# Splitting matmuls into 32-column tiles in a masked graph-attention layer

## The chip, the core and the metric

The kernel runs on one NeuronCore of a Trainium2 chip. The core has a matrix engine (TensorE, "PE" in the profile, whose weight loads stand apart as "PEld"), a vector engine (VectorE, "DVE"), an activation engine (ScalarE, "ACT"), a general engine (GpSimd, "POOL") and a sequencing engine that issues DMAs here (SyncE, "SP"). The metric is the device time of one execution in microseconds (us). The kernel before takes 3434.6 us (median of 5 runs, 3427.57 to 3441.34).

## The reference

The input x has 8 graphs of 2048 nodes and 256 channels in fp32; adj is a 2048 x 2048 integer matrix. One attention layer with 8 heads of 32 channels is followed by a feed-forward step, with three layer norms:

```python
qkv = einsum('fnc,ck->fnk', x, w_qkv); q, k, v = split(qkv, 3)
scores = einsum('fnhd,fmhd->fhnm', q, k) / sqrt(32)
scores = where(adj > 0, scores, -1e9)
attn = softmax(scores)
t = einsum('fhnm,fmhd->fnhd', attn, v)
y = layernorm(x + t) * g1 + be1
h = relu(y @ w1 + b1)
z = layernorm(y + h @ w2 + b2) * g2 + be2
out = layernorm(x + z)
```

All matrices of the layer are fp32 in the kernel as well, and all of its large products are fp32 matmuls.

## The kernel before, in words

**Items.** The attention is cut into 1024 items: 8 graphs (f), 4 chunks of 512 queries (qc), 2 groups of 4 heads (g) and 16 blocks of 128 keys (mb). All engines have their orders written out in one Python loop; no scheduler moves anything afterwards. In step t of the loop the kernel issues, in this order: one piece of other work (`advance`), the exponentials of item t + 1, the scores of item t + 2 (`LEAD = 2`), the values of item t, and the sums of its denominators (`add_up`).

**Scores** (L204 to L222). K and Q are held with channels on partitions, 32 channels to a head. For each of the four heads one product takes 32 rows of K (one head) by 128 keys as weights and streams the 512 queries: the result has 128 keys on partitions and 512 queries in a bank of PSUM. Two heads share a pair of banks. There are three pairs, used in turn, and an item takes two; so the scores of the next item can start when VectorE has read the first pair of the item before. VectorE adds the mask (L220, two instructions of 128 x 1024 an item) and writes the result to a buffer p in SBUF.

**Exponentials** (L224): one ScalarE instruction of 128 x 2048 an item, in place.

**Values** (L236): four products an item, one a head. The weights are 128 keys by 32 channels, and the result of head h goes to partitions 32h to 32h + 31 of one bank, which gathers over the 16 key blocks. The bank is one of two x banks, which change sides with every (f, qc, g).

**Denominators.** GpSimd (L258) and accumulating DMAs that GpSimd issues (L255) add up the exponentials of 16 items into four tiles; four products with a matrix of ones then sum over keys (L294, 128 rows by 32 columns each).

**Other work.** Generators hold the rest: transposes of x (`turn_rows`, L151), projections to Q and K (`channels`, L174) and V (`project`, L199), denominators (L294, L301), the division (L330), and a tail with layer norms, transposes (L396) and the feed-forward products (L409, L421). `advance` gives one piece of it to each step, between the values of one item and the scores of the next; a piece takes the free x bank. `MORE` marks a place where a piece may be cut in two. In the order of TensorE's work an item is therefore: scores, values, at most one such piece.

**Shapes on TensorE.** The scores use 32 rows by 128 columns of the array, the values and the ones 128 rows by 32 columns; projections, feed-forward products and transposes the whole 128 x 128.

The products in question, with the lines of the profile, and what calls them:

Of the kernel before, what the change touches and what calls it, by code (L numbers as in the profile page):

```python
# [19 lines left out]
P = 128  # L20
H = 8
D = 32
# [17 lines left out]
def stats(nc, small, t, mhalf):  # L40
    st = small.tile([P, nc.vector.BN_STATS_DIM], F32, name="st")
    nc.vector.bn_stats(st, t)
    mv = small.tile([P, nc.vector.BN_AGGR_DIM], F32, name="mv")
    nc.vector.bn_aggr(mv, st)
    rs = small.tile([P, 1], F32, name="rs")
    nc.gpsimd.tensor_scalar(rs, mv[:, 1:2], EPS, 1.0, op0=ALU.add, op1=ALU.mult)
    nc.gpsimd.tensor_tensor(rs, rs, mhalf, ALU.pow)
    return mv, rs


def normalize(nc, dst, t, mv, rs):
# [4 lines left out]
def fast_path(ctx, tc, cst, x, adj, out, RS):  # L56
    nc = tc.nc
    F, N, C = x.shape
    NCK, TPC, MB = N // CH, CH // P, N // P
# [19 lines left out]
    ident, identb, wqkv, w1s, w2s = cst["ident"], cst["identb"], cst["wqkv"], cst["w1s"], cst["w2s"]  # L79
    state = {"pair": 0, "side": None, "turn": 0, "turned": False, "holder": None, "tails": 0}  # L80

    def score_pair():
        i = state["pair"]
        state["pair"] = (i + 1) % 3
        return ps_s[i].tile([P, 2, CH], F32, name=f"s{i}")

    def bank(dt=F32):
        shape = [P, CH] if dt == F32 else [P, 2, CH]
        if state["side"] is not None:
            i = 1 - state["side"]  # L90
            return ps_x[i].tile(shape, dt, name=f"x{i}")
        i = state["turn"]
        state["turn"] = (i + 1) % 5
        pool = ps_s[i] if i < 3 else ps_x[i - 3]
        return pool.tile(shape, dt, name=f"s{i}" if i < 3 else f"x{i - 3}")
# [9 lines left out]
    def give(t):  # L105
        live[:] = [None if u is t else u for u in live]
# [32 lines left out]
    QT, KT, V, XT = {}, {}, {}, {}  # L139
    XD = [dp.tile([NCK, P, 2, CH], F32, name=f"xd{f}") for f in range(F)]  # L140

    def queries(f, c, xT):
        for g in range(2):
            yield from channels(QT, qp, "qT", (f, c, g), xT, g * P)
# [23 lines left out]
    def channels(store, pool, name, key, xT, k0):  # L168
        yield BANK
        ps = bank()  # L170
        for a in range(2):
            if a:
                yield MORE
            nc.tensor.matmul(ps, wqkv[:, a, k0:k0 + P], xT[:, a, :], start=(a == 0), stop=(a == 1))  # L174
        store[key] = pool.tile([P, CH], F32, name=name)
        nc.scalar.copy(store[key], ps)  # L176

    def reload(f, c):
        while (f, c) not in XT:
            yield 1  # L180
        yield INPUTS - 1
        xT = take([P, 2, CH], F32)
        nc.sync.dma_start(xT, XD[f][c])
        yield 3
        return xT

    def project(f, c, g, xT=None):
        if xT is None:
            xT = yield from reload(f, c)
            while len(KT) < (2 * f + g) * NCK + c:  # L190
                yield 1
        yield from channels(KT, kp, "kT", (f, c, g), xT, C + g * P)
        yield BANK
        ps = bank()
        for j in range(TPC):
            if j == TPC // 2:
                yield MORE
            for a in range(2):
                nc.tensor.matmul(ps[:, j * P:(j + 1) * P], xT[:, a, j * P:(j + 1) * P],  # L199
                                 wqkv[:, a, 2 * C + g * P:2 * C + (g + 1) * P], start=(a == 0), stop=(a == 1))  # L200
        v = vp.tile([P, TPC, P], F32, name="v")
        nc.scalar.copy(v, ps.rearrange("p (j c) -> p j c", c=P))
        V[f, c, g] = v
        give(xT)  # L204
# [4 lines left out]
    def scores(item):  # L209
        f, qc, g, mb = item  # L210
        pt = PT[item] = pp.tile([P, 4, CH], F32, name="p")
        ps2 = [score_pair() for _ in range(2)]

        for half in (1, 0):
            for j in range(2):
                r = D * (2 * half + j)
                nc.tensor.matmul(ps2[half][:, j, :], KT[f, mb // TPC, g][r:r + D, (mb % TPC) * P:(mb % TPC + 1) * P],  # L217
                                 QT[f, qc, g][r:r + D, :], start=True, stop=True)
        for half, ps in enumerate(ps2):
            nc.vector.tensor_tensor(pt[:, 2 * half:2 * half + 2, :], ps,  # L220
                                    MK[f, qc, mb // 2][:, mb % 2, None, :].to_broadcast([P, 2, CH]), ALU.add)
# [57 lines left out]
    def rows(v):  # L279
        return v[:, None, :].to_broadcast([P, TPC, C])  # L280
# [54 lines left out]
    def tail(f, qc, y, xin):  # L335
        yield from norm(y)
        yield from feed_forward(y)
        yield 1
        z = y
        yield from norm(z)  # L340
        nc.gpsimd.tensor_tensor(z, z, rows(cst["g2r"]), ALU.mult)  # L341
        yield 1
        nc.gpsimd.tensor_tensor(z, z, rows(cst["be2r"]), ALU.add)  # L343
        yield 1
        nc.gpsimd.dma_start(z, xin, accum_op=ALU.add)
        yield 7
        yield from norm(z)
        nc.sync.dma_start(out[f, qc * CH:(qc + 1) * CH, :].rearrange("(p j) c -> p j c", p=P), z)
        state["tails"] -= 1
# [20 lines left out]
    def finish(f, qc):  # L370
        y = yp.tile([P, TPC, C], F32, name="y")
        xr, xb = state["rows"], take([P, TPC, C], F32)
        yield from divide(f, qc, y)
        nc.vector.tensor_tensor(y, y, xr, ALU.add)
        norm_halves(y)
        nc.vector.tensor_tensor(xb, xr, rows(cst["be2r"]), ALU.add)
        yield from feed_forward(y)
        z = y
        norm_halves(z)
        for h in range(0, TPC, 2):  # L380
            nc.vector.tensor_tensor(z[:, h:h + 2], z[:, h:h + 2], rows(cst["g2r"])[:, h:h + 2], ALU.mult)
            nc.vector.tensor_tensor(z[:, h:h + 2], z[:, h:h + 2], xb[:, h:h + 2], ALU.add)
        norm_halves(z)
        dst = out[f, qc * CH:(qc + 1) * CH, :].rearrange("(p j) c -> p j c", p=P)
        for h in range(0, TPC, 2):
            nc.sync.dma_start(dst[:, h:h + 2], z[:, h:h + 2])

    def feed_forward(y):
        yield TURNED
        state["turned"] = True  # L390
        yT = work.tile([P, 2, CH], F32, name="turned")
        for a in range(2):
            yield BANK
            ps = bank()
            for j in range(TPC):
                nc.tensor.transpose(ps[:, j * P:(j + 1) * P], y[:, j, a * P:(a + 1) * P], ident)  # L396
            nc.scalar.activation(yT[:, a, :], ps, AF.Identity, bias=cst["be1c"][:, a:a + 1], scale=cst["g1c"][:, a:a + 1])
        yield 1
        nc.gpsimd.tensor_tensor(y, y, rows(cst["g1r"]), ALU.mult)
        yield 1  # L400
        nc.gpsimd.tensor_tensor(y, y, rows(cst["be1b2r"]), ALU.add)
        hT = work.tile([P, 2, CH], F32, name="hT")
        for d in range(2):
            yield BANK
            ps = bank()
            for a in range(2):
                if a:
                    yield MORE
                nc.tensor.matmul(ps, w1s[:, a, d * P:(d + 1) * P], yT[:, a, :], start=(a == 0), stop=(a == 1))  # L409
            nc.scalar.activation(hT[:, d, :], ps, AF.Relu, bias=cst["b1s"][:, d:d + 1], scale=1.0)  # L410
        state["turned"] = False
        yield 1
        z = y
        for jj in range(0, TPC, 2):
            yield BANK
            ps = bank()
            for j in range(jj, jj + 2):
                if j > jj:
                    yield MORE
                for d in range(2):  # L420
                    nc.tensor.matmul(ps[:, (j - jj) * C:(j - jj + 1) * C], hT[:, d, j * P:(j + 1) * P], w2s[:, d, :],  # L421
                                     start=(d == 0), stop=(d == 1))
            nc.vector.tensor_tensor(z[:, jj:jj + 2, :], ps.rearrange("p (b c) -> p b c", c=C), z[:, jj:jj + 2, :], ALU.add)


# [18 lines left out]
    def advance(t, free=True, finish=False):  # L444
# [18 lines left out]
        while state["holder"] and (finish or late and state["holder"][2] == MORE):  # L463
# [4 lines left out]


    NEXT = {(1, 1): [(turn, 0)], (3, 1): [(turn, 1)], (3, 10): [(project, 0, 0)], (5, 1): [(turn, 2)],  # L470
            (5, 8): [(project, 1, 0)], (6, 0): [(turn, 3)], (6, 4): [(project, 2, 0)], (6, 8): [(project, 3, 0)],
            (6, 12): [(project, 0, 1)], (7, 0): [(project, 1, 1)], (7, 4): [(project, 2, 1)], (7, 8): [(project, 3, 1)]}

    def begin():
# [324 lines left out]
```

## Time and profile before

| what | value |
|---|---|
| median of 5 runs | 3434.6 us |
| the profiled execution | 3435.5 us |
| its span, from the first to the last instruction | 3433.7 us |
| TensorE, share of the span | 93% |
| VectorE | 80% |
| GpSimd | 75% |
| ScalarE | 71% |
| granted clock of TensorE, share of full speed | 0.986 |
| DMA engines, 100 to 3380 us | 76% busy |

A group of the profile is written as line, engine, operation, what it writes and reads, shape and count, then the busy time of the group, the mean time of one instruction, and the time for which its engine was idle before it, with what ended the idle time. A matmul's shape is rows*columns of the array, then the streamed operand. The end of a matmul is modelled, so matmuls that follow each other overlap in the records by some 0.1 to 0.2 us; starts are measured. A line of the timeline is the start, the length, engine, line, operation, tiles, shape and the number of instructions merged. In the table of waits "A <- B" means that A's engine was idle until B was done. "PEldq" is TensorE's sequencer: EVENT_SEMAPHORE is an instruction of its own that only waits.

### The profile page before, as it was taken

Reading aid. Unit: us, or ns where it says so; the run is one execution under the profiler, and the core shown is the slowest. Engines: PE = TensorE matmul, PEld = TensorE weight load, DVE = VectorE, ACT = ScalarE, POOL = GpSimd, SP = SyncE. Lnnn points to the kernel's source line nnn. Section 1 sums busy time; section 2 is a strip of 40 time slices with the busy share of each in tenths; the row PEclk is TensorE's granted clock in tenths of the full one; section 3 lists DMA queues with packets and bytes.
Section 4 is the critical chain, followed back from the end, with each engine's and each line's share of the span. In section 5 each row is a group of like instructions: output and inputs, shape, how many; then the busy total and the mean of one; then the engine's idle time right before and its main releaser. Section 6 shows DMA issues by size and latency. Waiting matters only on the chain. (4 is left out here: it accounts for less than half of the span.)

```text
span 3433.7 us, 54404 instructions
## 1 busy us (share of the span) xinstructions
PE 3201.2 (93%) x22036; PEld 1033.9 (30%) x22036; DVE 2738.8 (80%) x3203; ACT 2427.1 (71%) x1937; POOL 2588.5 (75%) x1357
## 2 busy tenths in 40 slices
PE   6899999999998999989999999999999999999994
PEld 5222333223332233322332223323233223332222
DVE  4788878878778877888778788787877888788884
ACT  3677777767777777777777677676776777777773
POOL 0577778787787876887877787787887878787884
PEclk8999999999999999999999999999999999999997
DMA  8677778678678777778777778687787687787773
GB/s 307 141 161 172 173 168 182 149 153 199 149 171 170 164 175 171 165 153 183 172 166 160 163 172 185 142 175 163 169 186 158 150 181 176 169 170 153 152 155 87
DMA packets 149297, 575.98 MB, mean 168 GB/s; under 512 B 14608, under 2 KB 67344, under 8 KB 99888
## 3 DMA queue, kind: packets, MB, share of 16 engines
q0 software_dynamic: 64560, 435.85, 63.1%
q1 hardware_dynamic: 83664, 135.30, 11.7%
q8 instruction: 174, 2.85, 0.3%
q10 hardware_dynamic: 816, 1.31, 0.1%
q14 instruction: 83, 0.68, 0.1%
HBM read 131.99 MB, written 37.75 MB: 49 GB/s over the span
## 5 line engine op out<-in xcount | busy, mean ns | idle before, releaser
L220 DVE TENSOR_TENSOR p<-s,mask 128x1024 f32<-128x1024 f32 x2048 | 2410.9, 1219 | 558.8 <-PE s L217 334.5
L224 ACT ACTIVATE p<-p 128x2048 f32<-128x2048 f32 x1024 | 1956.1, 1910 | 535.0 <-DVE p L220 450.0
L258 POOL TENSOR_TENSOR p<-p 128x2048 f32<-128x2048 f32 x382 | 1814.4, 4753 | 315.1 <-ACT p L224 313.5
L217 PE MATMUL s<-qT,kT 32*128 32x512 f32 x8192 | 1173.7, 643 | 135.6 <-DVE p L220 129.9
L236 PE MATMUL x<-p,v 128*32 128x512 f32 x8192 | 1093.6, 606 | 3.3 <-ACT p L224 3.2
L255 POOL DMA_DIRECT2D p<-p x384 | 358.3, 989 | 418.0 <-DMA p<-p 170.6
L217 PEld LDWEIGHTS s<-qT,kT 32*128 32x128 f32 x8192 | 321.1, 183 | 741.1 <-DVE p L220 680.3
L236 PEld LDWEIGHTS x<-p,v 128*32 128x32 f32 x8192 | 161.3, 108 | 784.3 <-issue 283.0
L174 PE MATMUL x<-in,wqkv 128*128 128x512 f32 x472 | 255.5, 639 | 21.1 <-DMA in<-xd 16.3
L276 ACT ACTIVATE y<-y,nb,rs 128x256 f32<-128x256 f32 x372 | 219.4, 591 | 29.2 <-POOL nb L273 29.2
L294 PE MATMUL x<-p,ones 128*32 128x512 f32 x2016 | 239.3, 592 | 0.0
L265 DVE BATCH_NORM_STATS2 st<-y 128x6 f32<-128x256 f32 x372 | 155.2, 417 | 5.9 <-DMA y<-in_x_dram 5.9
L174 PEld LDWEIGHTS x<-in,wqkv 128*128 128x128 f32 x472 | 74.3, 189 | 204.8 <-issue 151.1
L421 PE MATMUL x<-w2s,hT 128*128 128x256 f32 x512 | 128.0, 392 | 0.0
L409 PE MATMUL x<-turned,w1s 128*128 128x512 f32 x248 | 127.3, 625 | 0.7 <-ACT hT L410 0.7
L296 ACT COPY dT<-x 128x512 f32<-128x512 f32 x63 | 36.9, 585 | 126.1 <-PE x L294 126.1
L199 PEld LDWEIGHTS x<-wqkv,in 128*128 128x128 f32 x896 | 105.8, 191 | 64.6 <-issue 35.2
L199 PE MATMUL x<-wqkv,in 128*128 128x128 f32 x896 | 120.5, 284 | 0.0
L421 PEld LDWEIGHTS x<-w2s,hT 128*128 128x128 f32 x512 | 91.9, 189 | 64.1 <-issue 50.8
L294 PEld LDWEIGHTS x<-p,ones 128*32 128x32 f32 x2016 | 65.5, 110 | 150.8 <-issue 150.5
L270 POOL TENSOR_TENSOR rs<-rs,mhalf 128x4 f32<-128x4 f32 x93 | 97.1, 1044 | 7.8
L176 ACT COPY kT<-x 128x512 f32<-128x512 f32 x59 | 34.5, 585 | 76.9 <-PE x L174 76.9
(117 smaller groups left out, 1433.4 us busy)
## 6 DMA issues: line engine op xcount, KB each, us to landing
p<-p POOLq DMA_DIRECT2D x384, 1024.0 KB, 10.4
mask<-md SPq DMA_DIRECT2D x248, 128.0 KB, 6.8
y<-in_x_dram POOLq DMA_DIRECT2D x62, 512.0 KB, 5.7
in<-xd SPq DMA_DIRECT2D x59, 512.0 KB, 10.2
p<-in_adj_dram SPq DMA_DIRECT2D x16, 1024.0 KB, 9.9
out_dram<-y SPq DMA_DIRECT2D x31, 512.0 KB, 3.0
in<-in_x_dram SPq DMA_DIRECT2D x29, 512.0 KB, 10.0
xd<-in SPq DMA_DIRECT2D x28, 512.0 KB, 7.7
```

The costliest lines, as they stand in the source:

```text
L174: nc.tensor.matmul(ps, wqkv[:, a, k0:k0 + P], xT[:, a, :], start=(a == 0), stop=(a == 1))
L199: nc.tensor.matmul(ps[:, j * P:(j + 1) * P], xT[:, a, j * P:(j + 1) * P], wqkv[:, a, 2 * C + g * P:2 * C + (g + 1) * P], start=(a == 0), s ...
L217: nc.tensor.matmul(ps2[half][:, j, :], KT[f, mb // TPC, g][r:r + D, (mb % TPC) * P:(mb % TPC + 1) * P], QT[f, qc, g][r:r + D, :], start=Tr ...
L220: nc.vector.tensor_tensor(pt[:, 2 * half:2 * half + 2, :], ps, MK[f, qc, mb // 2][:, mb % 2, None, :].to_broadcast([P, 2, CH]), ALU.add)
L224: nc.scalar.activation(PT[item], PT[item], AF.Exp, scale=1.0 / math.sqrt(D))
L236: nc.tensor.matmul(O[grp][r:r + D, :], V[f, mb // TPC, g][:, mb % TPC, r:r + D], PT[item][:, h, :], start=(mb == 0), stop=(mb == LAST))
L255: nc.gpsimd.dma_start(PT[f, qc, g, chain[0]], PT.pop(item), accum_op=ALU.add)
L258: nc.gpsimd.tensor_tensor(first, first, PT.pop(item), ALU.add)
L265: nc.vector.bn_stats(st, t[:, j, :])
L276: nc.scalar.activation(t[:, j, :], t[:, j, :], AF.Identity, bias=nb[:, j:j + 1], scale=rs[:, j:j + 1])
L294: nc.tensor.matmul(ps[r:r + D, :], cst["ones"], term[:, h, :], start=(n == 0), stop=(n == len(terms) - 1))
L421: nc.tensor.matmul(ps[:, (j - jj) * C:(j - jj + 1) * C], hT[:, d, j * P:(j + 1) * P], w2s[:, d, :], start=(d == 0), stop=(d == 1))
```

## The change

A new function splits a product by the columns of its weights: four matmuls, each with 32 columns of the weights, the same streamed operand, and a quarter of the partitions of the same result. The projections (Q, K, V) and the two feed-forward products call it, so that each 128 x 128 product becomes four of 128 rows by 32 columns. The scores call it for each head, so that a product of 32 x 128 becomes four of 32 x 32. Results, buffers and the order of everything else stay; the line numbers after L46 grow by 5, and all these matmuls then stand under the helper's line L53.

```diff
+def in_columns(nc, out, lhsT, rhs, start, stop):
+    for r in range(0, P, D):
+        nc.tensor.matmul(out[r:r + D], lhsT[:, r:r + D], rhs, start=start, stop=stop)
...
-            nc.tensor.matmul(ps, wqkv[:, a, k0:k0 + P], xT[:, a, :], start=(a == 0), stop=(a == 1))
+            in_columns(nc, ps, wqkv[:, a, k0:k0 + P], xT[:, a, :], start=(a == 0), stop=(a == 1))
...
-                nc.tensor.matmul(ps[:, j * P:(j + 1) * P], xT[:, a, j * P:(j + 1) * P],
-                                 wqkv[:, a, 2 * C + g * P:2 * C + (g + 1) * P], start=(a == 0), stop=(a == 1))
+                in_columns(nc, ps[:, j * P:(j + 1) * P], xT[:, a, j * P:(j + 1) * P],
+                           wqkv[:, a, 2 * C + g * P:2 * C + (g + 1) * P], start=(a == 0), stop=(a == 1))
...
-                nc.tensor.matmul(ps2[half][:, j, :], KT[f, mb // TPC, g][r:r + D, (mb % TPC) * P:(mb % TPC + 1) * P],
-                                 QT[f, qc, g][r:r + D, :], start=True, stop=True)
+                in_columns(nc, ps2[half][:, j, :], KT[f, mb // TPC, g][r:r + D, (mb % TPC) * P:(mb % TPC + 1) * P],
+                           QT[f, qc, g][r:r + D, :], start=True, stop=True)
...
-                nc.tensor.matmul(ps, w1s[:, a, d * P:(d + 1) * P], yT[:, a, :], start=(a == 0), stop=(a == 1))
+                in_columns(nc, ps, w1s[:, a, d * P:(d + 1) * P], yT[:, a, :], start=(a == 0), stop=(a == 1))
...
-                    nc.tensor.matmul(ps[:, (j - jj) * C:(j - jj + 1) * C], hT[:, d, j * P:(j + 1) * P], w2s[:, d, :],
-                                     start=(d == 0), stop=(d == 1))
+                    in_columns(nc, ps[:, (j - jj) * C:(j - jj + 1) * C], hT[:, d, j * P:(j + 1) * P], w2s[:, d, :],
+                               start=(d == 0), stop=(d == 1))
```

## The prediction

> **What bounds the kernel now.** I read the busy line and the groups first, then the timeline of TensorE in a quiet stretch, then single groups and windows.
>
> ```profile
> PE 3201.2 (93%) x22036; PEld 1033.9 (30%) x22036; DVE 2738.8 (80%) x3203; ACT 2427.1 (71%) x1937; POOL 2588.5 (75%) x1357
> L217 PE MATMUL s<-qT,kT 32*128 32x512 f32 x8192 | 1173.7, 643 | 135.6 <-DVE p L220 129.9
> L236 PE MATMUL x<-p,v 128*32 128x512 f32 x8192 | 1093.6, 606 | 3.3 <-ACT p L224 3.2
> L174 PE MATMUL x<-in,wqkv 128*128 128x512 f32 x472 | 255.5, 639 | 21.1 <-DMA in<-xd 16.3
> L421 PE MATMUL x<-w2s,hT 128*128 128x256 f32 x512 | 128.0, 392 | 0.0
> q8 instruction: 174, 2.85, 0.3%
> ```
>
> TensorE is busy 93% of the span and waits little. There are 1024 items (8 graphs, 4 query chunks, 2 head groups, 16 key blocks), and 8192 records at L217 for 4096 products: each fp32 product is two weight loads and two matmuls, here called two passes. Timeline, TensorE alone:
>
> ```profile
> 1009.68 1.14 PE L217 MATMUL s<-qT,kT 32*128 32x512 f32 x8
> 1010.75 1.06 PE L236 MATMUL x<-p,v 128*32 128x512 f32 x8
> 1011.74 1.12 PE L409 MATMUL x<-turned,w1s 128*128 128x512 f32 x2
> 1012.80 1.14 PE L217 MATMUL s<-qT,kT 32*128 32x512 f32 x8
> ...
> 1015.35 1.14 PE L217 MATMUL s<-qT,kT 32*128 32x512 f32 x8 [0.41 <-DVE p L220]
> ...
> 1022.66 1.07 PE L236 MATMUL x<-p,v 128*32 128x512 f32 x8
> 1023.66 1.99 PE L421 MATMUL x<-w2s,hT 128*128 128x256 f32 x8
> 1025.58 1.14 PE L217 MATMUL s<-qT,kT 32*128 32x512 f32 x8
> ...
> 1030.64 1.06 PE L236 MATMUL x<-p,v 128*32 128x512 f32 x8
> 1031.53 1.90 PE L294 MATMUL x<-p,ones 128*32 128x512 f32 x16
> 1033.36 1.14 PE L217 MATMUL s<-qT,kT 32*128 32x512 f32 x8
> ```
>
> An item is scores, values, and at most one piece of other work (a "fill"), back to back. The values take 0.99 us before a fill of another tile shape (1010.75 to 1011.74), but 0.89 before the denominator's ones (1030.64 to 1031.53), which have the same shape, 128 rows by 32 columns. So a change of shape costs 0.10 us. The items without a fill last 2.55 us (1012.80 to 1015.35) and end with a wait for VectorE.
>
> Now single passes:
>
> ```profile
> 1500.37 0.61 PE L217 MATMUL s<-qT,kT 32*128 32x512 f32 x4
> 1500.90 0.64 PE L236 MATMUL x<-p,v 128*32 128x512 f32 x4
> ```
>
> These are the second pass of four score tiles and the first pass of four value tiles. Four matmuls of 587 and 617 ns lie within 0.61 and 0.64 us, so the four tiles run together, each starting 7 ns after the one before. The score group began at 1499.83: to its second pass 0.54 us, from there to the values 0.53. The values' second pass starts at 1501.36, 0.46 later. With a pass of 0.43 us (0.89 = two passes and a load of 0.03), a 128-column load stands open for 0.11 us, a 32-column load for 0.03, and draining before the next shape costs 0.10.
>
> Last, the sequencer, which hands TensorE its instructions:
>
> ```profile
> L174 PEldq EVENT_SEMAPHORE  x1: 51/51/51, 462.4 to 462.4; - x1
> L217 PEld LDWEIGHTS s<-qT,kT x8: 181/182/184, 462.3 to 462.5; 32*128 32x128 f32 x8
> L151 PEldq EVENT_SEMAPHORE  x1: 51/51/51, 7.5 to 7.5; - x1
> L174 PEldq EVENT_SEMAPHORE  x1: 51/51/51, 7.6 to 7.6; - x1
> ```
>
> At 462.4 the sequencer takes up a wait that lies behind 16 score and 16 value instructions, just as the first score tiles start; 77 of the 163 such waits after the opening stand at this same point. So about 32 instructions are held ahead, not more. At the start it handles one wait at 7.5, then 16 instructions, then another at 7.6 (85 ns between them in the trace): at most 5 ns an instruction, 9 by the rounded figures.
>
> **The change, part by part.** No instruction moves on any engine and no wait or DMA is added; SP, POOL, ACT and DVE issue the same list. Only products are split: on TensorE 24,576 matmuls more for scores and 6,912 for the rest (512 + 1024 + 256 + 512, three more each), as many weight loads, so 22,036 becomes some 53,500.
>
> (1) Projections and feed-forward (L174, L199, L409, L421) become four tiles of 128x32, the shape of the values. Gone are the shape change between values and fill (0.10) and most of the open load (0.11); passes stay. From the rows: values plus four passes of 512 columns take 2.72 us in one shape (1030.64 to 1033.36) and 2.92 in two (1022.66 to 1025.58; L421's eight passes of 256 are the same columns): 0.20 saved. With one product: 2.05 (1010.75 to 1012.80) against 2.72 less two passes, 1.86: 0.19 saved. In the timeline I count 410 such fills behind values (L174 191, L409 78, L199 77, L421 64): 410 x 0.195 = 80 us. The opening stretch (to 60 us), where these products stand beside transposes of 128x128, waits for DMA and VectorE; I cost its added shape changes at nothing, at most 16 x 2 x 0.10 = 3 us if that cover is gone.
>
> What is late next is VectorE:
>
> ```profile
> 1009.68:1012.80 3.12, 3.12 (x19) 0.77 (x19) 2.35 (x3) 2.36 (x2) 3.12 (x2) 1.00 1.10 236
> 1021.59:1025.58 3.99, 3.99 (x25) 1.90 (x24) 2.87 (x3) 2.77 (x3) 3.08 (x2) 1.00 0.00 0
> ```
>
> Columns: stretch, its length, busy time of PE, weight loads, DVE, ACT, POOL. Items with such a fill leave VectorE 0.8 to 1.1 us free, far over 0.2. A few carry extra VectorE work; I let 5% go: 76 us gained. Bounds: 83, and 60 if a quarter of the items had no slack.
>
> (2) Scores: 16 tiles of 32x32 instead of four of 32x128, 64 instructions instead of 16. The open load shrinks from 0.11 to 0.03 (-0.08). The last tile starts later: before, 3 x 7 = 20 ns after the first; now 15 x 7 = 100 ns if all 64 instructions are at hand. But 32 are, and the last tile's first is number 61: 28 more have to come. At 0 ns each 0.10 us is the end from below; at 5 ns, with 26 ns for the first to arrive (from the end of the wait at 7.5 to the next weight load), 0.17; at 9 ns 0.28. I take 0.14, by a price just under the 5 ns that the trace gives as a maximum. So a score group changes by -0.08 + (0.14 - 0.02) = +0.04 us; ends 0.00 and +0.18. It lies on the path of every item: TensorE is the bound with a fill, and without one VectorE's first addition needs the last score tile, and the next scores need that addition. 1024 x 0.04 = 41 us lost; ends 0 and 184.
>
> (3) Instruction fetch doubles from 2.85 MB; 0.3% of the DMA engines' span becomes 0.7%. Nothing, as POOL and the queues have slack at 75% busy.
>
> Sum against the profiled execution, 3435.5 us (span 3433.7; the median is 3434.6): 3435.5 - 76 + 41 = 3400 us.
>
> [...]
>
> [...]
>
> **The rivals.**
> A, slower: the feed of the scores decides. If the last tile starts more than 76/1024 + 0.10 = 0.174 us after the first, the loss exceeds the gain; at 0.28 us the time is 3435.5 - 76 + 184 = 3544. For it: 32 held ahead, 5 ns is close to the limit. Against: 5 ns is an upper bound.
> B, slower by far: tiles of one row strip do not all run side by side. No row shows a 32x32 tile, nor more than four at once, and the two passes of a tile stand together in the stream, so 12 waiting second passes might block the rest. In two batches a score group has a third pass in line: 0.43 x 1024 = 440, 3800 us. In four batches, three more: 4680. Against: row tiles and column tiles each overlap cleanly.
> C, no change: feed cost and gain cancel (last tile at 0.16 to 0.18 us), or VectorE takes the place of TensorE in the fills: 3425 to 3445.
> D, the change does nothing because column tiles run one after another: excluded by the four value matmuls in 0.64 us.
>
> **How the numbers follow.** Forecast 0.57, C 0.11, A 0.16, B 0.16. The forecast alone runs from 3352 (83 gained, nothing lost) to 3425. The range holds the forecast, C and A up to its bound: 3345 to 3550, 0.84 less a little at its edges. Faster 0.57, same 0.11, slower 0.32; 0.3%, 10 us, is about what a measurement of this kernel can tell from no change.
>
> **What the profile after would show.** The projections with 128*32 in their form; values to fill in 0.89 us instead of 0.99; fills without an open load. Scores with 32*32, x32 in the timeline; from their start to the values 1.11 us (1.07 before), 1.07 or less if the queue holds them all, 1.5 or more if B. Items without a fill would go from 2.55 to 2.59. The prediction is wrong if score groups grow by over 0.08 us, or if the time of the fills comes back as a wait of L217 for L220.

## The result, and the profile after

The changed kernel takes 3450.6 us (median of 28 runs, 3440.3 to 3458.8) against 3435.8 us (54 runs) for the kernel before on the same chips. The ratio is 1.0039 with a 95% interval of 1.0030 to 1.0047: slower by 0.4%, some 13 us. The forecast was 3400 us and faster; its range, 3345 to 3550, holds the time, and the chance given to "slower" was 0.32. The profiled execution took 3458.9 us, with a span of 3457.1 and a granted clock of 0.981; it is 8 us slower than the median, and sums over its trace are that much too long.

The page of the changed kernel: engines, the instruction queue (packets, MB, share), and three groups (line, engine, operation, tiles, shape and count, then busy us and mean ns, then the idle time before them and what ended most of it).

```profile
PE 3181.9 (92%) x53524; PEld 929.9 (27%) x53524; DVE 2738.4 (79%) x3203; ACT 2432.9 (70%) x1937; POOL 2600.9 (75%) x1357
q8 instruction: 421, 6.90, 0.8%
L225 DVE TENSOR_TENSOR p<-s,mask 128x1024 f32<-128x1024 f32 x2048 | 2410.6, 1219 | 599.8 <-PE s L53 390.0
L53 PE MATMUL s<-qT,kT 32*32 32x512 f32 x32768 | 1210.1, 604 | 161.3 <-DVE p L225 140.8
L53 PE MATMUL x<-in,wqkv 128*32 128x512 f32 x1888 | 248.4, 603 | 24.2 <-DMA in<-xd 23.2
```

The tiles are there: 53,524 matmuls, as counted. TensorE is not fuller. VectorE (L225) waits 390.0 us for scores; before, it was 334.5.

TensorE alone, in a stretch with projections (timeline: start, length, engine, line, operation, shape, instructions merged), then an item without a fill, from one score group to the next:

```profile
1504.70 1.08 PE L241 MATMUL x<-p,v 128*32 128x512 f32 x8
1505.59 1.06 PE L53 MATMUL x<-in,wqkv 128*32 128x512 f32 x8
1506.58 1.14 PE L53 MATMUL s<-qT,kT 32*32 32x512 f32 x32
1507.65 1.08 PE L241 MATMUL x<-p,v 128*32 128x512 f32 x8
...
2311.18 1.15 PE L53 MATMUL s<-qT,kT 32*32 32x512 f32 x32 [0.51 <-DVE p L225]
...
2313.84 1.15 PE L53 MATMUL s<-qT,kT 32*32 32x512 f32 x32 [0.51 <-DVE p L225]
```

Values to fill take 0.89 us (1504.70 to 1505.59), as predicted. Scores to values take 1.07 (1506.58 to 1507.65): the 16 score tiles do run side by side. But an item without a fill now lasts 2.66 us (2311.18 to 2313.84), where it lasted 2.55 and 2.59 was predicted, and it still ends with TensorE waiting for VectorE.

From the starts of the score groups in the two traces I worked out the time of an item by the work that lies in it:

| in the item | items | median before, us | after | sum before, us | after |
|---|---|---|---|---|---|
| no fill | 245 | 2.545 | 2.665 | 642.6 | 685.5 |
| projection to Q or K | 191 | 3.123 | 2.942 | 663.6 | 649.9 |
| projection to V | 77 | 3.155 | 2.957 | 274.2 | 263.5 |
| first feed-forward product | 76 | 3.980 | 3.800 | 278.2 | 270.8 |
| second | 63 | 3.991 | 3.810 | 246.5 | 236.4 |
| transposes of y | 62 | 2.655 | 2.672 | 166.6 | 183.7 |

The rest (ones, other transposes) is 7 us longer together. By medians every fill is 0.18 to 0.20 us shorter, 407 of them, but their sums fall by 42 us only: single long waits make up the difference. Items without a fill lose 43 us, of which their median explains 29 (245 x 0.12); transposes of y lose 17, of which theirs explains 1. Most of the remainder is the kind of wait that comes next.

One kind of long wait was not in any rival. Timeline of TensorE and VectorE, after a V projection:

```profile
2140.07 1.95 PE L53 MATMUL x<-wqkv,in 128*32 128x128 f32 x64
2141.95 1.13 PE L53 MATMUL s<-qT,kT 32*32 32x512 f32 x31
2145.10 0.79 PE L53 MATMUL s<-qT,kT 32*32 32x512 f32 x1 [2.01 <-issue]
...
2145.93 1.22 DVE L225 TENSOR_TENSOR p<-s,mask 128x1024 f32<-128x1024 f32 x1 [3.57 <-PE s L53]
```

Of 32 score matmuls 31 start, and the last one comes 3 us after the first, although it waits for nothing ("issue"). Take as a break more than 0.5 us between the starts of two successive weight loads or matmuls of one group of scores or values, behind 100 us and at a granted clock over 0.9. There are 20 such breaks, 25.6 us in all, the longest 3.0 us, and none in the trace of before. Each goes on 1.27 to 1.59 us after a packet of the instruction queue has ended. (The expectations below count 25 broken groups and 36.7 us.)

Some of these waits are paid twice: behind them the granted clock of TensorE is at half for some microseconds, 0.50 from 2105 to 2110 us for example, behind a break of 3.0 us. TensorE is busy for 75.2 us at half clock in the changed kernel, against 43.0 before, so up to 16 us of the time, by estimate, is this.

So three theories stand to be told apart. **Completion:** VectorE sees the end of 16 tiles later than that of four. **Fetch:** TensorE runs out of instructions. **Transfers and waits:** the saving of the fills runs into something other than TensorE. The expectations name theories by letters: C is completion; N, F and G are about the number of instructions and their fetch; W, D and V are about waits.

### The profile page after: what moved, and what is told of

It is laid out like the page before. It is cut to its first block, busy times and chain, and to the rows that moved or that the text cites. A ratio compares the mean times of both kernels' runs of the same rounds, so it can differ in the third digit from the quotient of the medians.

```text
span 3457.1 us, 117380 instructions
## 1 busy us (share of the span) xinstructions
PE 3181.9 (92%) x53524; PEld 929.9 (27%) x53524; DVE 2738.4 (79%) x3203; ACT 2432.9 (70%) x1937; POOL 2600.9 (75%) x1357
## 5 line engine op out<-in xcount | busy, mean ns | idle before, releaser
L225 DVE TENSOR_TENSOR p<-s,mask 128x1024 f32<-128x1024 f32 x2048 | 2410.6, 1219 | 599.8 <-PE s L53 390.0
L53 PE MATMUL s<-qT,kT 32*32 32x512 f32 x32768 | 1210.1, 604 | 161.3 <-DVE p L225 140.8
L53 PEld LDWEIGHTS s<-qT,kT 32*32 32x32 f32 x32768 | 252.0, 103 | 822.5 <-DVE p L225 740.5
L53 PE MATMUL x<-in,wqkv 128*32 128x512 f32 x1888 | 248.4, 603 | 24.2 <-DMA in<-xd 23.2
L53 PE MATMUL x<-w2s,hT 128*32 128x256 f32 x2048 | 122.8, 379 | 0.4 <-ACT hT L415 0.4
L53 PE MATMUL x<-turned,w1s 128*32 128x512 f32 x992 | 122.5, 597 | 0.0
L53 PEld LDWEIGHTS x<-wqkv,in 128*32 128x32 f32 x3584 | 103.3, 110 | 44.9 <-issue 30.8
L53 PE MATMUL x<-wqkv,in 128*32 128x128 f32 x3584 | 114.3, 273 | 0.2 <-issue 0.2
L53 PEld LDWEIGHTS x<-in,wqkv 128*32 128x32 f32 x1888 | 67.1, 111 | 166.5 <-issue 150.8
L53 PEld LDWEIGHTS x<-w2s,hT 128*32 128x32 f32 x2048 | 67.8, 110 | 70.9 <-issue 35.5
L406 POOL TENSOR_TENSOR y<-y,be1b2r 128x1024 f32<-128x1024 f32 x32 | 85.4, 2669 | 0.1
```

What stands on the lines that cost most here:

```text
L53: nc.tensor.matmul(out[r:r + D], lhsT[:, r:r + D], rhs, start=start, stop=stop)
```

## The experiments

### Each half alone

The scores alone, on the kernel before:

```diff
-                nc.tensor.matmul(ps2[half][:, j, :], KT[f, mb // TPC, g][r:r + D, ...], QT[f, qc, g][r:r + D, :],
-                                 start=True, stop=True)
+                in_columns(nc, ps2[half][:, j, :], KT[f, mb // TPC, g][r:r + D, ...], QT[f, qc, g][r:r + D, :],
+                           start=True, stop=True)
```

> Before's projections and feed-forward products, one 128x128 tile each; only the scores are 16 tiles of 32x32. Theory C: every item whose next scores wait for VectorE's first addition is 0.12 us longer: 245 items with no fill, and some part of the 250 with transposes or sums, so 30 to 60 us: 3465 to 3495 us. The fill items, whose next scores come 0.69 us after that addition's end, get only the 12 ns by which the values start later. Scores' start to VectorE 1.387 us, to the values 1.083. Theory W: the scores cost only those 12 ns an item, 6 us in all: 3435 to 3445 us. Theory N: 24,576 more matmuls at some ns each that the queue does not hide; with the 15 us by which the changed kernel is slower plus 76 saved, divided by its three quarters, 3435 + 68: 3500 us, with longer TensorE groups everywhere, fill items too.

Measured: 3484.2 us against 3441.9 for the kernel before, ratio 1.0120 (1.0103 to 1.0137): 42 us slower. The trace of this kernel, scores and the addition that waits for them, above those of the kernel before:

```profile
1871.97 1.14 PE L53 MATMUL s<-qT,kT 32*32 32x512 f32 x32
1873.37 2.35 DVE L225 TENSOR_TENSOR p<-s,mask 128x1024 f32<-128x1024 f32 x2 [0.80 <-PE s L53]
```

```profile
1906.53 1.14 PE L217 MATMUL s<-qT,kT 32*128 32x512 f32 x8
...
1907.80 2.36 DVE L220 TENSOR_TENSOR p<-s,mask 128x1024 f32<-128x1024 f32 x2 [1.43 <-PE s L217]
```

1.40 us against 1.27; the medians over items without a fill are 1.386 and 1.265. To the values it is 1.083 and 1.071. The first matmul of the last tile starts 100 to 115 ns after that of the first tile, but the shorter weight load makes up for it (103 ns at the mean in this kernel, 183 in the kernel before): the last matmul of the group starts 0.553 to 0.566 us after the first, and 0.553 before. The 0.12 us lie behind that start: 0.820 to 0.832 us to VectorE where it was 0.712. So TensorE itself is hardly delayed; what VectorE waits for is. Completion holds: items without a fill are 2.664 us at the median, and no group is broken by the measure above.

The fills alone, with the scores undivided (the changed kernel with the edit above taken back):

> The projections and feed-forward products stay four 128x32 tiles, the scores go back to four 32x128 tiles, one matmul a head. Theory C (completion): what slowed the changed kernel is that VectorE's first addition starts 0.12 us later after a group of 16 score tiles; the fills' saving of 0.19 to 0.20 us is real. Then this kernel has the scores' start to VectorE back at 1.267 us, items without a fill at 2.55 us, fill items at about 2.96 (projections) and 3.81 us (feed-forward), and takes 3350 to 3375 us (3435.5 less most of the 76 us of the prediction). Theory W (waits): the fills' saving comes back as waits of TensorE for ScalarE's exponentials and VectorE whatever the scores look like; then 3425 to 3440 us, as before. Theory N (number of instructions): time goes with the count of matmuls, and three quarters of the added ones are the scores'; the fills' quarter of the cost is left, some 5 to 10 us, less the saving: also well under 3400 us.

Measured: 3398.1 us, ratio 0.9879 (0.9862 to 0.9896): 42 us faster. The fill items are at 2.925 us (Q, K), 2.941 (V), 3.783 and 3.793 (feed-forward), items without a fill back at 2.546, and no group is broken. Single items are as theory C expected; the time is not. By medians 407 fill items save 82 us, and the sums of the trace save 51 on them. The time lies between the ranges of theories C and W. These views show where the saving stops, in the trace of this kernel (timeline; the DMA view of the same stretch with size and us from issue to landing; waits of the whole trace with us in total, times, longest):

```profile
2314.07 1.93 PE L53 MATMUL x<-in,wqkv 128*32 128x512 f32 x8 [8.60 <-DMA in<-xd]
```

```profile
in<-xd SPq DMA_DIRECT2D x1, 512.0 KB, 23.0
```

```profile
POOL p L260 <- DMA p<-p: 244.4, 62, 9.2
...
PE s L222 <- DVE p L225: 129.3, 269, 3.4
...
ACT y L281 <- POOL nb L278: 57.2, 20, 9.3
...
PE x L53 <- DMA in<-xd: 30.9, 9, 8.6
...
PE x L241 <- ACT p L229: 20.9, 21, 2.9
```

A projection waits 8.6 us for its reloaded input; TensorE's waits for reloads are 30.9 us in all, and 16.3 before. Its waits for exponentials at the values are 20.9 us, and 3.2 before. Its wait for VectorE at the scores has not grown (129.3 and 129.9). Two queues upstream are later as well: GpSimd waits 244.4 us for the transfers that it issues to add up the exponentials (170.6 before), and ScalarE 57.2 us for GpSimd at the layer norms (29.2 before). The DMA engines' busy share, with all their packets, is full from 2291 to 2314 us (1.04 of the stretch), while that reload is under way.

The two halves together would be zero by these runs (-42 + 42); the whole change is +13. So the halves also cost something jointly.

### How the completion depends on the tiles

Two tiles of 32x64 for each score product, eight instead of 16; and 16 tiles with the columns in the outer loop:

```diff
-def in_columns(nc, out, lhsT, rhs, start, stop):
-    for r in range(0, P, D):
-        nc.tensor.matmul(out[r:r + D], lhsT[:, r:r + D], rhs, start=start, stop=stop)
+def in_columns(nc, out, lhsT, rhs, start, stop, w=D):
+    for r in range(0, P, w):
+        nc.tensor.matmul(out[r:r + w], lhsT[:, r:r + w], rhs, start=start, stop=stop)
...
-                           QT[f, qc, g][r:r + D, :], start=True, stop=True)
+                           QT[f, qc, g][r:r + D, :], start=True, stop=True, w=2 * D)
```

> The changed kernel with each score product as two tiles of 32x64 (8 matmuls a group in place of 16); the fills stay four 128x32. Theory C: end of the last stream to VectorE's start is about 193 ns + 9 ns a tile (four tiles 228, sixteen 336), so 264 ns for eight; the open weight load is 54 ns (107 for 128 columns, 27 for 32) and the last tile starts about 47 ns after the first. So the scores' start to VectorE is 1.267 - 0.053 + 0.027 + 0.036 = 1.277 us, and to the values about 1.05; items without a fill 2.55 to 2.56 us; 3345 to 3375 us, within 15 us of the kernel with the scores undivided. Theory W: 3435 or more. Theory N: half of the scores' added instructions are left (8,192 of 24,576): a third of what separates the changed kernel from the one with undivided scores.

```diff
-        for half in (1, 0):
-            for j in range(2):
-                r = D * (2 * half + j)
-                in_columns(nc, ps2[half][:, j, :], ...)
+        for c in range(0, P, D):
+            for half in (1, 0):
+                for j in range(2):
+                    r = D * (2 * half + j)
+                    k0 = (mb % TPC) * P + c
+                    nc.tensor.matmul(ps2[half][c:c + D, j, :], KT[f, mb // TPC, g][r:r + D, k0:k0 + D], ...)
```

> The changed kernel with its 16 score tiles in another order: the four heads inside, the columns outside, so that successive matmuls go to successive row groups and to another bank. Theory C with a cost per tile: nothing changes, the last stream's end to VectorE stays 336 ns, scores' start to VectorE 1.39 us, 3440 to 3460 us. If the late completion comes from four tiles one after the other in the same row group (a group's second passes running one after the other), the end falls towards 228 ns and the time to about 3380 to 3400 us.

With eight tiles: 3395.9 us, ratio 0.9866 (0.9849 to 0.9882), the time of undivided scores. Its trace:

```profile
1815.36 1.11 PE L53 MATMUL s<-qT,kT 32*64 32x512 f32 x16
1816.64 2.35 DVE L225 TENSOR_TENSOR p<-s,mask 128x1024 f32<-128x1024 f32 x2 [0.53 <-PE s L53]
```

Scores to VectorE 1.28 us (median 1.279, expected 1.277), to the values 1.045, items without a fill 2.559. From the start of the last matmul to VectorE the medians are 0.712 us with four tiles, 0.752 with eight and 0.820 to 0.832 with 16: 9 to 10 ns for each tile. The single number expected for the time, 3345 to 3375, was missed together with that of the fills.

With the other order: 3452.1 us, ratio 1.0039 (1.0024 to 1.0054), like the changed kernel, and 0.820 us from the last matmul's start. The order doesn't matter. In these four kernels the tiles get narrower as they get more, so width would be a rival to number. The second feed-forward product, which VectorE also reads, settles it: from its last matmul's start to VectorE it takes 418 ns with one tile of 128 columns, 427 with two of 64 and 448 with four of 32 (before, the 64-column fills below, and the fills alone). Tiles of 32 columns cost 30 ns where they are three more, and 108 to 120 ns where they are 12 more: it is the number.

### What the saving in a fill is made of

Fills in two tiles of 128x64, scores undivided:

```diff
-    for r in range(0, P, D):
-        nc.tensor.matmul(out[r:r + D], lhsT[:, r:r + D], rhs, start=start, stop=stop)
+    for r in range(0, P, 2 * D):
+        nc.tensor.matmul(out[r:r + 2 * D], lhsT[:, r:r + 2 * D], rhs, start=start, stop=stop)
```

> The fills (projections and feed-forward) as two tiles of 128x64 instead of four of 128x32; the scores undivided. Step 1 of the prediction put the saving of 0.20 us a fill down to two things: 0.10 us for a change of tile shape against the values, and 0.11 us of open weight load of which 0.03 is left. If that is right, the change of shape stays with 64 columns (values to fill 0.99 us) and only half of the open load goes: 0.04 to 0.06 us a fill, so the items with one product of a projection fall from 3.12 to about 3.07 us instead of 2.93, and the time is 3415 to 3430 us, within 10 to 25 us of before. If any split in columns lets the fill run on from the values, the saving is 0.15 us and more a fill, items 2.95 us, and the time is about that of the fills with 32 columns, 3395 to 3410 us.

Measured: 3432.0 us, ratio 0.9976 (0.9952 to 1.0000). TensorE's timeline:

```profile
1007.43 1.07 PE L241 MATMUL x<-p,v 128*32 128x512 f32 x8
1008.43 1.08 PE L53 MATMUL x<-turned,w1s 128*64 128x512 f32 x4
1009.44 1.14 PE L222 MATMUL s<-qT,kT 32*128 32x512 f32 x8
```

Values to fill 1.00 us, fill to scores 1.01; items with Q or K 3.076 us, 0.047 less than before. The price of the change of shape stays whole with 64 columns, and half of the open load is gone, as step 1 of the prediction has it. The saving of 0.20 us needs the shape of the values. The time is 2 us over the expected range: 407 fills times 0.047 us are 19 us, and by the ratio 8 arrive.

### The broken groups

The changed kernel, with the V projections undivided:

```diff
-                in_columns(nc, ps[:, j * P:(j + 1) * P], xT[:, a, j * P:(j + 1) * P],
+                nc.tensor.matmul(ps[:, j * P:(j + 1) * P], xT[:, a, j * P:(j + 1) * P],
                            wqkv[:, a, 2 * C + g * P:2 * C + (g + 1) * P], start=(a == 0), stop=(a == 1))
```

> The changed kernel with the V projections (L204) back to one 128x128 product; everything else stays divided, the 16 score tiles too. In the changed kernel's trace 25 groups of scores or values are broken apart for 0.5 to 3.5 us (36.7 us in all) with nothing that they wait for, and each goes on 1.27 to 1.59 us after a packet of the instruction queue has ended; the kernel with only the fills divided has none, the one with only the scores divided has one. Theory F (fetch): a V projection in tiles is 128 instructions on TensorE in 1.95 us, followed by 64 for the scores, and there instructions run out. Whole, it is 32; the instructions of the whole program fall by only 6% (48 products more per group and pass, 64 groups: 6.90 MB to about 6.5). Then the broken groups fall from 25 to under 8, and the time is 3450 less 25 to 35, plus up to 15 us (77 items with 0.20 us of saving given up): 3430 to 3445 us. Theory G: it is the total of instructions that matters; then 20 or more groups stay broken and the time is 3450 to 3465 us.

Measured: 3437.2 us, ratio 0.9989 (0.9971 to 1.0007). Its instruction queue and the waits of VectorE:

```profile
q8 instruction: 397, 6.50, 0.7%
```

```profile
DVE p L225 <- PE s L53: 353.9, 445, 6.6
```

One break is left of 20, with 6% fewer instruction bytes, so it is the dense place and not the total: 18 of the 20 come in an item with a V projection or within two items after it. In ratios the kernel is 17 us faster than the changed one (0.0050 of 3440, give or take 7 us) although the V items are 12 us longer (275.4 against 263.5): the broken groups cost about 29 us, the half clock behind them included.

That it is the fetch can be put in numbers of the traces. The change adds 2 x 31,488 instructions and 4.05 MB (6.90 less 2.85), so 64 bytes each; a packet of 16,384 bytes holds 256. Number the records of TensorE in the order of time, its weight loads, matmuls and sequencer's waits: each of the 20 breaks of the changed kernel comes behind a record whose number, divided by 256, leaves 193. So does each of the 19 breaks with the columns outside, of the 13 with fewer transfers (below), and the one left here. All 53 stand at the end of a packet.

Why the next packet isn't there in time is a matter of some 5 us. In the changed kernel a packet's transfer starts 2.7 us (median) after TensorE has begun with the packet before it, takes 0.95 us, and its instructions are used 1.2 us after it has ended at the earliest. A V projection in tiles is 128 instructions in 1.9 us, with the scores and values of its item 208 in 3.83 (2138.12 to 2141.95 in the changed kernel), a rate at which a packet lasts 4.7 us; an item without a fill has 80 in 2.66 us, and a packet lasts 8.5. In before, each packet has ended at least 12.6 us before its first instruction starts. Why a transfer starts when it does, these runs don't show.

### The transfers

The last accumulating transfer of each chain left out, in the kernel before, in the one with the fills divided, and in the changed kernel. The denominators of these three lack two of 16 blocks; they serve for their times alone:

```diff
-            if mb in chain[1:]:
+            if mb in chain[1:3]:
                 nc.gpsimd.dma_start(PT[f, qc, g, chain[0]], PT.pop(item), accum_op=ALU.add)
+            if mb == chain[3]:
+                PT.pop(item)
```

> The kernel before with the last accumulating transfer of each chain left out, so that 256 of 384 transfers of 1 MB remain and two of 16 blocks are missing in the denominators. It is the base for the next two kernels, with less traffic on the DMA engines. In before TensorE waits only 16.3 us for the reloaded inputs; 3395 to 3432 us.

> The kernel with only the fills divided, with the same transfers left out (two of 16 blocks missing in the denominators). With all transfers the division of the fills gained 42 us, where the medians of the items say 82. Theory D (transfers): the rest went into waits for inputs and buffers that come through full DMA engines (the first projection after a reload waits up to 9.5 us, and TensorE's long waits grew by 24 us). Then this kernel is 60 to 80 us faster than the one before with the same transfers left out. Theory V: the rest went into the additions of VectorE and the exponentials of ScalarE, whatever the DMA engines do: 35 to 48 us faster.

> The changed kernel, scores and fills divided, with the same transfers left out (two of 16 blocks missing in the denominators). If the broken groups come from instruction packets that stand behind full DMA engines, they fall from 25 to under 8, and the kernel is 15 to 40 us faster than the one before with the same transfers left out (60 to 80 gained in the fills, 42 lost in the scores). If the fetch is late by itself, 20 or more groups stay broken and the kernel is within 15 us of it.

Measured: 3408.7, 3342.7 and 3414.7 us (ratios to before 0.9912, 0.9711 and 0.9928; intervals 0.9883 to 0.9942, 0.9681 to 0.9741, 0.9906 to 0.9950). With fewer transfers the fills gain 66 us instead of 42 (by the intervals 55 to 84 instead of 36 to 47). GpSimd's wait for its transfers in the first of these kernels, then three waits in the second:

```profile
POOL p L255 <- DMA p<-p: 7.6, 4, 3.2
```

```profile
PE x L53 <- DMA in<-xd: 18.0, 6, 5.3
...
POOL p L260 <- DMA p<-p: 5.6, 4, 1.6
...
PE x L241 <- ACT p L229: 0.4, 1, 0.4
```

TensorE's waits for exponentials are gone (0.4 us for 20.9 with all transfers), and those for reloads are 18.0 for 30.9: so the transfers are behind the saving that didn't arrive, the exponentials' part of it above all.

The third is 6 us slower than the first, and 13 breaks stay (16.8 us), between the two expectations. Fewer transfers take away a third of them, and the packets take 0.95 to 0.96 us at the median in each of these traces, so full DMA engines are not the main cause. The parts now add up: -66 for the fills, +42 for the scores and +29 for broken groups are +5; measured +6. But +42 and +29 were measured with all transfers, and the intervals are some 10 us wide on each side, so that they agree to 1 us is luck. With all transfers the same sum, -42 + 42 + 29, is +29, and measured is +13. Some 16 us of the later scores and broken groups fall into time in which the transfers were late anyway; that is argued from this sum, and the runs don't show it directly.

### Which transfers

Two attempts to let the fills' saving through with complete results. One of six accumulating transfers given to GpSimd:

```diff
-    POOLED = (0, 3, 6, 8, 11, 13, 15)
-    MOVED = ((1, 4, 7, 10), (2, 5, 9, 12))
+    POOLED = (0, 3, 6, 8, 10, 11, 13, 15)
+    MOVED = ((1, 4, 7), (2, 5, 9, 12))
```

> The kernel with only the fills divided, with one of the six accumulating transfers of a group given to GpSimd instead (block 10 added to its own chain); the result is complete. By the runs with fewer transfers, the DMA engines stand in the way of the fills' saving: there 66 us of it arrived instead of 42. If relief of the DMA engines is enough, this kernel takes 3370 to 3390 us (one transfer of six instead of two taken away: half of the 28 us by which the kernel before got faster, and half of the 24 us more of saving). Against it: GpSimd gets 64 additions of 4.8 us, 307 us, and goes from 76% to about 86% busy; if its additions come late, buffers and the layer norms that it computes are late too, and the kernel takes 3398 us or more.

And eight items instead of three between a reload and its projection, with divided fills and in the kernel before:

```diff
         nc.sync.dma_start(xT, XD[f][c])
-        yield 3
+        yield 8
```

> The kernel with only the fills divided, and between the reload of an input chunk and the first projection that reads it 8 items instead of 3, so some 23 us instead of 9. In the kernel with the fills divided TensorE waits 30.9 us for these reloads (9 times, up to 8.6 us), and one that was issued at 2290.95 landed after 23 us. If it is the late reload that keeps part of the fills' saving from arriving, the wait falls to under 8 us and the time from 3398 to 3365 to 3385 us. If the time waits for the DMA engines anyway (buffers of exponentials, GpSimd), the wait moves to another line and the time stays at 3390 to 3405 us; the longer hold of the two input buffers could also push the projections together at the end of a graph, over 3405 us.

> The kernel before with the same 8 items between reload and projection. It waits 16.3 us for reloads, so 3420 to 3435 us; the distance to the kernel with divided fills and early reloads tells whether the fills' saving (42 us with late reloads, 66 with a third of the transfers left out) arrives: 55 us or more if the reload was what stood in its way, 38 to 48 if not.

The first: 3399.8 us, ratio 0.9878 (0.9857 to 0.9900), nothing gained over 3398.1. The waits of this kernel:

```profile
PE x L53 <- DMA in<-xd: 47.1, 13, 9.2
...
POOL p L260 <- DMA p<-p: 21.9, 16, 3.1
```

GpSimd's wait for transfers is nearly gone, 21.9 us of 244.4 (it is 83% busy instead of 77), and the projections wait for reloads longer. By the sums over items, those with the first feed-forward product are 10 us shorter than with the fills alone, those without a fill 5, and those with Q or K 18 us longer: what one wait gives back the other takes.

The second: 3431.7 us (ratio 0.9977, 0.9966 to 0.9988) and 3474.2 us (1.0091, 1.0073 to 1.0109). No wait for a reload is left in either trace, and both are over 33 us slower than without the edit; held buffers change which pieces of work lie in which item (70 items with a V projection instead of 77). The first lies over 3405 us, where its expectation put a case of its own; the second misses its range. The distance between them is 42 us, as with late reloads. In the trace of the first of them the wait has moved to ScalarE and the values:

```profile
2779.37 0.60 ACT L281 ACTIVATE y<-y,nb,rs 128x256 f32<-128x256 f32 x1 [6.08 <-POOL nb L278]
2779.88 1.89 ACT L229 ACTIVATE p<-p 128x2048 f32<-128x2048 f32 x1
...
2781.82 1.20 PE L241 MATMUL x<-p,v 128*32 128x512 f32 x8 [4.28 <-ACT p L229]
```

A layer norm on ScalarE waits 6.08 us for GpSimd, the next exponentials stand behind it, and the values behind those. So neither the reload alone nor GpSimd's wait for its transfers alone is what keeps the saving back; with either gone, the other wait or the exponentials hold TensorE. Leaving transfers out relieves all of them at once (GpSimd also issues 128 transfers fewer), and more of the saving arrives. Which of them ends last in which stretch stays open.

## Why the prediction was wrong

**Step 1, the fills: the size was right, what comes next was not.** 0.195 us a fill was predicted, 0.197 to 0.214 is measured with undivided scores, and its two parts are confirmed by the 64-column fills. "What is late next is VectorE", with 0.8 to 1.1 us of slack, was the step that failed: VectorE had that slack (TensorE waits 129.3 us for it at the scores with divided fills, 129.9 before), but the reloads had none, nor had the exponentials, which wait behind the transfers that sum them. TensorE's waits for reloads grew from 16.3 to 30.9 us and those for exponentials from 3.2 to 20.9, together 32 us. Of 76 us 42 arrived. The profile of before had signs of it: a wait of 170.6 us of GpSimd for its own transfers, and L174 waiting for `in<-xd`. The prediction took 75% busy over the whole span for slack, where the stretch that mattered is full.

**Step 2, the scores: 41 us predicted, 42 measured, for another reason.** The open load shrank as expected (the second pass of the score tiles starts 0.453 us after the first in the changed kernel, and 0.533 before), and the last tile starts 0.10 to 0.115 us after the first where I took 0.14. The prediction's end from below, 0.10 us with all 64 instructions at hand, was nearer to the measurement. How many instructions are held ahead the runs don't settle; with 32, as the prediction estimates from the wait at 462.4, the 28 that had to come cost nearly nothing. So a group costs TensorE 0.012 us, not 0.04, and over 1024 items that is 12 us. What I left out is the completion: 0.12 us from the scores to VectorE instead of the same 0.012. It counts where the prediction said, in items without a fill (245 x 0.12 = 29 us), and not in fill items, where the next scores come 0.69 us after VectorE's first addition has ended. A right sum, then, by two errors that offset each other, so by luck. These 41 us go by medians; in the sums of the trace with the scores alone, items without a fill are 22 us longer and those with Q or K 14, because single long waits shift between them.

**Step 3, the instruction fetch: "nothing" was wrong, about 29 us.** I weighed bytes against the DMA engines' time, 0.7%, and 0.8% is what the page shows. What decides is whether the next packet is there when 208 instructions go in 3.8 us: all breaks stand at the end of a packet.

The sum: the 48 us between the forecast of -35 and the measured +13 are 34 us of the fills' saving that didn't arrive, 1 on the scores, and 13 that remain for the broken groups. The 13 are a remainder and not a measurement; alone, the breaks cost about 29.

**The rivals.** A needed the last tile to start 0.174 us after the first: refuted. B, tiles one after another: refuted, scores to values 1.083 us instead of 1.5. C named the right kind of loss, something else taking TensorE's place in the fills, but the wrong engine. No rival held the completion or the fetch. Neither of the two signs of being wrong came: scores to values grew by 0.012 us, not by over 0.08, and TensorE's wait for VectorE at the scores by 11 us (129.9 to 140.8). What did show it was an expected value, items without a fill: 2.66 us instead of 2.59.

## What to carry to other kernels

Tiles side by side were nearly free for TensorE here (0.012 us a group), but not for whoever reads the product (0.12): measure from the first matmul to the reader's start, and divide only as far as the shape change saves something. Here fills of four tiles and score products of two took 3395.9 us, 1.3% less than before, where 16 score tiles gave it all back. For the instruction fetch look at the place with most instructions per microsecond, not at the sum of bytes. For transfers look at the fullest stretch of the DMA engines, not at their mean.

## What the runs showed of the hardware

- The end of a group is seen 9 to 10 ns later for each fp32 tile in it (0.712, 0.752 and 0.820 to 0.832 us from the last start for 4, 8 and 16 tiles; 418, 427 and 448 ns for 1, 2 and 4 in the second feed-forward product), in both orders that were run.
- Sixteen fp32 tiles of 32x32, 32 matmuls in all, run side by side: the last starts 100 to 115 ns after the first, and the next product 1.071 to 1.083 us after it.
- From values of 128x32 to a product of 128x64 it takes 1.00 us, to one of 128x128 0.99, and to one of their own shape 0.89: the change of shape costs 0.10 to 0.11.
- TensorE ran out of instructions in the middle of a group, for up to 3.0 us, always at the end of a packet of 256 instructions. A packet takes 0.95 us, and TensorE goes on 1.3 to 1.6 us after it has ended.
- Behind some long waits of TensorE its granted clock is at half (0.50 from 2105 to 2110 us in the changed kernel, whose trace has 12 such stretches of 3.4 or 6.8 us between 100 and 3400 us; all begin after the start of a wait of 1.1 to 8.5 us, by 0.6 to 5.3 us).
